# A graph product of 15 batches as seven block products, with layernorm and row sums in other bursts

## The chip, the cores and the metric

The kernel runs on one core of one Trainium2 chip. The metric is device time in microseconds (us) of one execution, lower is better. The core's engines are TensorE (PE in the profile, with its weight loads shown apart as PEld), VectorE (DVE), ScalarE (ACT), GpSimd (POOL) and SyncE (SP, which here only issues DMAs). Each engine runs its own instructions in order; they meet through semaphores. All data are float32.

## The reference

The input is x of 16 batches, each 1024 nodes (N) by 256 channels (C), and one 1024 x 1024 adjacency matrix. Layer 0 is an attention whose queries come from a graph product; layer 1 is a graph convolution with two batch norms. Cut to what matters here:

```python
fea = jnp.transpose(x, (0, 2, 1))                       # [B, C, N]
c_adj = jnp.mean(fea, axis=1)                           # mean over channels, [B, N]
diff = c_adj[:, None, :] - c_adj[:, :, None]
A = jnp.abs(jnp.abs(jax.nn.sigmoid(diff) - 0.5) - 0.5) * 2.0
Wg = adj[None] * (A + jnp.transpose(A, (0, 2, 1))) * 0.5
g = jnp.einsum('bcn,bnm->bcm', fea, Wg)                 # the graph product
q = jax.nn.relu(g * para)                               # queries
k, v = split(x @ kv_w)                                  # 4 heads of 64 channels
attn = jax.nn.softmax(q @ k.T * scale)                  # per head, 1024 x 1024
x = layernorm(x + attn @ v)
# layer 1
x = layernorm(x + batchnorm(relu(batchnorm(A_hat @ x @ W1.T)) @ W2.T))
```

The graph product of one batch is a 256 x 1024 matrix times a 1024 x 1024 matrix. It is the part that is changed.

## The kernel before

**Stages.** The attention of all 16 batches comes first, up to about 1640 us of the span. Layer 1 follows and is untouched by the change. The order of work on TensorE, ScalarE, VectorE and SP in the attention stage is written out by hand: the program's order is the order in which each of these engines (and the SP queue of DMA issues) executes. GpSimd is scheduled separately.

**Bursts.** One unit is a 128 x 1024 tile of scores (128 keys, two heads of 512 queries each). A burst is two units, and a batch has 16 bursts, numbered u = 0 to 15 (the loop at L1266). In every burst the order is: `scores` of this burst's two units (L944: matmuls into `ps`, then ScalarE's exponential into `p`), then `back`, which is `outputs` of the burst before (L960: matmuls of `p` with the values into `po`, then VectorE's running sum `acc` of `p`, L981 and L983). `ps` has two PSUM buffers of two banks each (tag "s"), `p` has four SBUF buffers. A third pair of PSUM buffers of one bank each (tag "t", `tile_t`) serves everything else. After bursts 3, 7, 11 and 15 a group of eight units is complete: in the following burst `po` is copied by ScalarE (L990), added and transposed in 32 x 32 squares by VectorE (L991, L1001), stored (L1002) and later read back as rows (L1011). `normalise` (L1013) makes the denominators with one small matmul group `den`, sends them through HBM and back to columns; `residual` (L1038) divides and adds to x, on GpSimd.

**What prepares the next batch.** While batch b's bursts run, batch b+1's (and the start of b+2's) preparation is spread over them by `prologue` (L774), which returns three lists:

- `first`: `begin` (L784) sums x over channels on VectorE (L788), stores the 1024 means to HBM in 4-byte pieces (L795) and reads them back as a row on all partitions, `crow` (L797); `transpose_squares` (L810) transposes x from a second load `xS` in 32 x 32 squares (`load_squares`, L758, four DMAs for each half of the channels, one buffer).
- `side`: for each of eight 128-row blocks, `weights_abs` (L833) and `weights_tanh` (L838) on ScalarE and `weights_adj` (L842) on VectorE, which give `wg`, the weighted adjacency. The first needs `crow`.
- `steps`: values and keys from xT (L889, L902), and the graph product (L846): for each half c of the channels, eight blocks by two halves of 512 columns, 16 matmuls into a `tile_s` pair, followed by one VectorE operation times `para` (L861) and one rectifier on ScalarE (L864).

**Where they run, for batch b:** burst 0: values and keys of b+1, side entries; bursts 1 to 3: the remaining side entries; burst 4: the layernorm of batch b-1 (`statistics_x1` and `finish_x1`), the first half of the graph product of b+1 and the last keys; burst 5: load of x and of the first squares for b+2; burst 8: `begin` and the first transpose for b+2, the second half of the graph product of b+1, `normalise`; bursts 9 to 15: side entries for b+2, one or two per burst; burst 11: `residual` and the second transpose.

Batch 0's own graph product is a separate routine (`graph_first`, L866) and stays as it is.

Of the kernel before, what the change touches and what calls it, by code (L numbers as in the profile page):

```python
# [10 lines left out]
F32 = mybir.dt.float32  # L11
I32 = mybir.dt.int32
AF = mybir.ActivationFunctionType
ALU = mybir.AluOpType
# [4 lines left out]
P = 128  # L19
# [496 lines left out]
def fast_path(  # L516
# [187 lines left out]
    H0, H1 = slice(0, HALF), slice(HALF, N)  # L704
    C0, C1 = slice(0, P), slice(P, C)
# [27 lines left out]
    with (  # L733
# [12 lines left out]
        st = {}  # L746
# [27 lines left out]
        def prologue(b):  # L774
# [6 lines left out]
            def step(f, *a):  # L781
                steps.append((f, a))
# [27 lines left out]
            def transpose_squares(c):  # L810
                if c == 0:
                    s["xT"] = xTp.tile([P, CC, N], F32, tag="xT", name=f"xT_{b}")
                nc.vector.transpose(
                    s["xT"][:, c, :], s["xS", c].rearrange("p j i -> p (j i)")
                )
                if c == 0:
                    load_squares(b, 1)

            def row_of_means():

# [22 lines left out]
                    w, w, 1.0, adj_s[:, n, :], op0=ALU.subtract, op1=ALU.mult  # L843
                )

            def graph_mm(c, n):  # L846
                if n == 0:
                    s["pg"] = tile_s(f"pg_{b}_{c}")
                    if c == 0:
                        s["qT"] = qkv.tile([P, CC, N], F32, tag="qT", name=f"qT_{b}")  # L850
                for hs in (H0, H1):
                    nc.tensor.matmul(  # L852
                        s["pg"][:, hs], xt[:, n, c * P : (c + 1) * P], s["wg", n][:, hs],
                        start=(n == 0), stop=(n == NCH - 1),
                    )
                if n == NCH - 1:
                    queries(c, slice(0, N), s["pg"])

            def queries(c, hs, ps):
                q = s["qT"][:, c, hs]  # L860
                nc.vector.scalar_tensor_tensor(  # L861
                    q, ps, -scale, para_s[:, c, hs], op0=ALU.mult, op1=ALU.mult
                )
                nc.scalar.activation(q, q, AF.Relu)  # L864
# [56 lines left out]
            for c in range(CC if b else 0):  # L921
                for n in range(NCH):
                    step(graph_mm, c, n)
            for n in range(NCH if b == 0 else 0):
                step(graph_first, n)
            for n in range(NCH):
                side.append((weights_abs, (n,)))
                side.append((weights_tanh, (n,)))
                if n:
                    side.append((weights_adj, (n - 1,)))  # L930
            side.append((weights_adj, (NCH - 1,)))
            return first, steps, side


# [136 lines left out]
        def run(fs, k):  # L1071
            for f, a in fs[:k]:
                f(*a)
            del fs[:k]
# [129 lines left out]
        with tc.manual_schedule(  # L1204
# [61 lines left out]
            for j in range(len(bursts)):  # L1266
                b, u = j // PERB, j % PERB
                for i in bursts[j]:
                    scores(i)
                if u == 0:  # L1270
                    steps, side = next_steps, next_side
                    next_first, next_steps, next_side = [], [], []
                if j:
                    back(j - 1)
                if u in (5, 9, 13):
                    run(rows_of, 1)
                if u == 5 and b + 2 < B:
                    load_x(b + 2)
                    load_squares(b + 2, 0)
                    next_first, next_steps, next_side = prologue(b + 2)  # L1280
                if b == B - 1:
                    if u == 0:
                        run(sums, 1)
                        run(rows_of, 1)
                    elif u in (2, 13):
                        run(full, 2)
                    elif u == 8:
                        run(sums, 1)
                    elif u == 3:
                        late.clear()  # L1290
                elif u == 0:
                    for i in range(7):
                        if b:
                            run(steps, 1)
                            if i < 5:
                                run(side, 2)
                        if i == 1:
                            run(sums, 1)
                            run(rows_of, 1)
                elif u < 4:  # L1300
                    if u == 1:
                        run(full, 2)
                    run(side, 2 if u < 3 else 99)
                elif u == 4:
                    run(late, 1)
                    keys_last = steps[:1] if b else []
                    del steps[: len(keys_last)]
                    for n in range(NCH):
# [610 lines left out]
```

## Time and profile before

| What | Time |
|---|---|
| median of 3 runs | 2533.0 us (2530.41 to 2534.95) |
| the profiled execution | 2533.89 us |
| its span, first to last instruction | 2532.1 us |
| its mean granted TensorE clock | 0.996 |

| Engine | busy us | share |
|---|---|---|
| VectorE | 1606.9 | 63% |
| ScalarE | 1197.5 | 47% |
| GpSimd | 415.6 | 16% |

| Line | what | count | busy us, mean ns |
|---|---|---|---|
| L973 | matmuls of p with values | 4096 | 506.6, 589 |
| L952 | matmuls of scores | 4096 | 504.9, 593 |
| L983 | VectorE, running sum of p | 384 | 505.4, 1316 |
| L842 | VectorE, weights times adjacency | 128 | 161.4, 1281 |
| L833 | ScalarE, absolute value | 128 | 146.7, 1147 |
| L838 | ScalarE, tanh | 128 | 135.8, 1061 |

A float32 matmul shows as two records, each of about half its time; four 64 x 64 matmuls share the array in L952 and L973. Matmul records overlap, so their mean durations are longer than their spacing. The second of the profile's tables splits the span in 40 slices; the DMA engines are lightly loaded in the attention stage and SP's issue order matters more than bandwidth.

### The profile page before, as it was taken

To read this page: it belongs to the slowest core of one execution; us is meant where nothing else is said; L and a number is where in the kernel's file an instruction comes from. 1 tells how busy PE (TensorE), PEld (TensorE's weight loads), DVE (VectorE), ACT (ScalarE), POOL (GpSimd) and SP (SyncE) were. 2 spreads that over 40 slices of the span, in tenths; PEclk is the share of its full clock that TensorE was granted. 3 is DMA by queue.
4 is the path that set the end of the run, shared out by engine and by line. 5 is a ranking of instruction groups with operands and counts; after the bars stand their busy time and mean duration, and the time that the engine had idled before them with its cause. 6 is when DMAs were issued, how large, how long until landed. Compare 5 with 4: busy or idle time off the path is not lost.

```text
span 2532.1 us, 32436 instructions
## 1 busy us (share of the span) xinstructions
PE 2493.3 (98%) x12646; PEld 1085.3 (43%) x12646; DVE 1606.9 (63%) x2082; ACT 1197.5 (47%) x1471; POOL 415.6 (16%) x486
## 2 busy tenths in 40 slices
PE   9999999999999999999999999999999999999997
PEld 5443443434444434434444443344444444444455
DVE  5475665765756656657657566865655566468568
ACT  6375664654755656646647555510110110144458
POOL 0011110101111111102011112431222122000026
PEclk9999999999999999999999999999999999999999
DMA  3123223132232232231322312222221222165559
GB/s 133 38 41 81 60 43 73 45 64 59 47 76 63 39 76 66 45 71 34 76 59 43 80 34 43 76 71 95 84 100 67 87 96 100 63 219 166 183 174 342
DMA packets 396978, 216.19 MB, mean 85 GB/s; under 512 B 335504, under 2 KB 368784, under 8 KB 388368
## 3 DMA queue, kind: packets, MB, share of 16 engines
q1 hardware_dynamic: 391456, 163.16, 26.0%
q0 software_dynamic: 4832, 50.34, 4.8%
q8 instruction: 101, 1.65, 0.3%
q14 instruction: 61, 0.50, 0.1%
q10 hardware_dynamic: 528, 0.52, 0.1%
HBM read 130.29 MB, written 83.69 MB: 85 GB/s over the span
## 4 chain that ended last, share of the span: by engine, by line
PE 84%; DVE 11%; DMA 2%; issue 1%; ACT 1%; SPq 1%; POOL 0%; DVEq 0%; POOLq 0%; ACTq 0%
PE ps L952 16%; PE po L973 16%; PE pg L852 15%; PE pv L902 5%; PE b_agg L1424 4%; PE pk L889 4%; PE c_agg L1424 4%; PE po L1706 3%; PE a_agg L1424 2%; PE b_h L1456 2%; PE b_o L1632 2%; PE c_h L1456 2%; PE c_o L1632 1%; PE a_h L1456 1%; PE pg L874 1%
## 5 line engine op out<-in xcount | busy, mean ns | idle before, releaser
L983 DVE TENSOR_TENSOR acc<-acc,p 128x1024 f32<-128x1024 f32 x384 | 505.4, 1316 | 146.3 <-ACT p L957 120.7
L957 ACT ACTIVATE p<-ps 128x1024 f32<-128x1024 f32 x512 | 495.9, 1021 | 155.7 <-PE ps L952 106.6
L973 PE MATMUL po<-p,v 64*64 64x512 f32 x4096 | 506.6, 589 | 1.3 <-DVE oT L991 1.3
L952 PE MATMUL ps<-qT,kT 64*64 64x512 f32 x4096 | 504.9, 593 | 2.1 <-ACT p L957 1.8
L852 PE MATMUL pg<-wg,x 128*128 128x512 f32 x960 | 420.0, 595 | 0.0
L973 PEld LDWEIGHTS po<-p,v 64*64 64x64 f32 x4096 | 172.8, 133 | 277.0 <-issue 261.5
L852 PEld LDWEIGHTS pg<-wg,x 128*128 128x128 f32 x960 | 179.9, 190 | 239.6 <-issue 215.3
L952 PEld LDWEIGHTS ps<-qT,kT 64*64 64x64 f32 x4096 | 160.2, 133 | 282.2 <-issue 217.2
L1047 POOL TENSOR_TENSOR o<-o,r_all 128x512 f32<-128x512 f32 x62 | 77.4, 1249 | 1078.5 <-DVE r_all L1041 885.3
L861 DVE SCALAR_TENSOR_TENSOR qT<-pg,para_s 128x1024 f32<-128x1024 f32 (+1 forms) x34 | 39.2, 1161 | 248.8 <-PE pg L852 246.0
L842 DVE SCALAR_TENSOR_TENSOR wg<-wg,adj_s 128x1024 f32<-128x1024 f32 x128 | 161.4, 1281 | 18.4 <-ACT wg L838 18.4
L864 ACT ACTIVATE qT<-qT 128x1024 f32<-128x1024 f32 (+1 forms) x34 | 34.2, 1009 | 264.4 <-DVE qT L861 264.4
L833 ACT ACTIVATE wg<-crow,ccol 128x1024 f32<-128x1024 f32 x128 | 146.7, 1147 | 11.4 <-DMA crow<-c 11.1
L838 ACT ACTIVATE wg<-wg 128x1024 f32<-128x1024 f32 x128 | 135.8, 1061 | 1.8
L902 PE MATMUL pv<-kvw_s,xT 128*128 128x256 f32 x512 | 123.9, 385 | 0.0
L889 PE MATMUL pk<-xT,kvw_s 128*128 128x512 f32 x256 | 121.9, 598 | 0.0
L630 ACT ACTIVATE x<-x,nm_l,rs_l 128x256 f32<-128x256 f32 x128 | 64.9, 590 | 119.9 <-POOL nm_l L626 119.9
L902 PEld LDWEIGHTS pv<-kvw_s,xT 128*128 128x128 f32 x512 | 95.0, 190 | 50.2 <-issue 28.3
L1424 PE MATMUL a_agg<-ahT,x1l 128*128 128x512 f32 x240 | 108.1, 593 | 0.7 <-ACT agg L1192 0.7
L1424 PE MATMUL b_agg<-aT,x1S 128*128 128x512 f32 x240 | 107.9, 592 | 0.0
L1048 POOL TENSOR_TENSOR x<-x,o 128x512 f32<-128x512 f32 x62 | 97.5, 1573 | 4.7
L656 ACT COPY p_agg<-a_agg 128x512 f32<-128x512 f32 x15 | 8.8, 586 | 183.3 <-PE a_agg L1424 183.3
(208 smaller groups left out, 2863.5 us busy)
## 6 DMA issues: line engine op xcount, KB each, us to landing
h<-hw POOLq DMA_DIRECT2D x16, 2048.0 KB, 6.6
hl<-h SPq DMA_DIRECT2D x32, 1024.0 KB
x<-x POOLq DMA_DIRECT2D x16, 1024.0 KB, 4.2
x1l<-x SPq DMA_DIRECT2D x16, 1024.0 KB
xf<-x SPq DMA_DIRECT2D x16, 1024.0 KB
o<-oS SPq DMA_DIRECT2D x62, 256.0 KB
o<-o SPq DMA_DIRECT2D x248, 64.0 KB
x<-in_x_dram SPq DMA_DIRECT2D x15, 1024.0 KB
```

The lines of the kernel that those rows point to most:

```text
L833: nc.scalar.activation(w, s["crow"], AF.Abs, bias=s["ccol"][:, n : n + 1])
L838: nc.scalar.activation(w, w, AF.Tanh, scale=0.5)
L842: nc.vector.scalar_tensor_tensor(w, w, 1.0, adj_s[:, n, :], op0=ALU.subtract, op1=ALU.mult)
L852: nc.tensor.matmul(s["pg"][:, hs], xt[:, n, c * P : (c + 1) * P], s["wg", n][:, hs], start=(n == 0), stop=(n == NCH - 1),)
L889: nc.tensor.matmul(ps, kvw_s[:, c, kc * P : (kc + 1) * P], s["xT"][:, c, hs], start=(c == 0), stop=(c == CC - 1),)
L902: nc.tensor.matmul(pt[:, j * C : (j + 1) * C], s["xT"][:, c, n * P : (n + 1) * P], kvw_s[:, c, C : 2 * C], start=(c == 0), stop=(c == CC - 1),
L952: nc.tensor.matmul(ps[kh * D : (kh + 1) * D, hd * HALF : (hd + 1) * HALF], kT[r, pr, ks], qT[r, pr, qh * HALF : (qh + 1) * HALF], start=Tr ...
L957: nc.scalar.activation(p, ps, AF.Exp)
L973: nc.tensor.matmul(g["po"][kh][hd * D : (hd + 1) * D, :], s["v"][r, m, h * D : (h + 1) * D], p[r, hd * HALF : (hd + 1) * HALF], start=(m = ...
L983: nc.vector.tensor_add(g["acc"], g["acc"], p)
L1424: nc.tensor.matmul(ps, left, right, start=(start and i == 0), stop=(i == NCH // 2 - 1), skip_group_check=True,)
L1456: nc.tensor.matmul(ps, left, right, start=start, stop=True, skip_group_check=True)
```

## The change

The 256 x 1024 by 1024 x 1024 product of batches 1 to 15 is written in two-by-two blocks: the left matrix in four blocks A11 to A22 (512 nodes by 128 channels), the right one in four blocks of `wg` (512 x 512: `lo` and `hi` rows, H0 and H1 columns). Seven block products replace the eight of before; each is four matmuls into one PSUM bank of tag "t". The sums that this takes are made in place by VectorE: the left ones in a buffer S that shares the one buffer of `xS`, the right ones over the blocks of `wg` themselves, in four rounds `right(1)` to `right(4)`, each as soon as the products that read the old contents are past. Products 1 and 2 add up in bank a, product 3 takes d, products 6, 7 and 4 add up in bank b, product 5 takes c. Partial results are kept in qT.

The work around it is placed anew. The load of x goes from burst 5 to 7, the first squares from 5 to 9, the second from 8 to 12; `begin` goes from 8 to 10, the two transposes from 8 and 11 to 12 and 15. The side entries of batches from 2 on go from bursts 9 to 15 and 0 to 2 to bursts 12 to 15 (three in each) and burst 0 (two with each of the first six steps), in a new order with ScalarE's entries ahead. The layernorm of the batch before is cut in four parts, in bursts 2, 3, 5 and 6.

```diff
             def transpose_squares(c):
...
-                if c == 0:
-                    load_squares(b, 1)
...
-            def graph_mm(c, n):
-                if n == 0:
-                    s["pg"] = tile_s(f"pg_{b}_{c}")
...
-                for hs in (H0, H1):
+            A11, A12 = xt[:, M0, C0], xt[:, M1, C0]
+            A21, A22 = xt[:, M0, C1], xt[:, M1, C1]
...
+            def left_first():
+                s["S"] = xsp.tile([P, 2, NCH // 2, P], F32, tag="xS", name=f"S_{b}")
+                s2, s4 = s["S"][:, 0], s["S"][:, 1]
+                nc.vector.tensor_tensor(s2, A21, A22, ALU.add)
+                nc.vector.tensor_tensor(s2, s2, A11, ALU.subtract)
+                nc.vector.tensor_tensor(s4, A12, s2, ALU.subtract)
+
+            def left_third():
+                nc.vector.tensor_tensor(s["S"][:, 1], A11, A21, ALU.subtract)
+
+            def left_last():
+                nc.vector.tensor_tensor(s["S"][:, 0], A21, A22, ALU.add)
+
+            def right(k):
+                for i in KC:
+                    dst, one, two = {
+                        1: (lo(i, H1), lo(i, H1), lo(i, H0)),
+                        2: (hi(i, H1), hi(i, H1), lo(i, H1)),
+                        3: (lo(i, H0), hi(i, H1), lo(i, H0)),
+                        4: (hi(i, H0), hi(i, H0), hi(i, H1)),
+                    }[k]
+                    nc.vector.tensor_tensor(dst, one, two, ALU.subtract)
+
+            def product(k, ps, start):
+                S = s["S"]
+                for i in KC:
+                    left, right = {
+                        1: (xt[:, i, C0], lo(i, H0)),
+                        2: (xt[:, i + NCH // 2, C0], hi(i, H0)),
+                        3: (S[:, 1, i], hi(i, H1)),
+                        4: (xt[:, i + NCH // 2, C1], hi(i, H0)),
+                        5: (S[:, 0, i], lo(i, H1)),
+                        6: (S[:, 0, i], hi(i, H1)),
+                        7: (S[:, 1, i], lo(i, H0)),
+                    }[k]
                     nc.tensor.matmul(
-                        s["pg"][:, hs], xt[:, n, c * P : (c + 1) * P], s["wg", n][:, hs],
-                        start=(n == 0), stop=(n == NCH - 1),
-                    )
-                if n == NCH - 1:
-                    queries(c, slice(0, N), s["pg"])
+                        ps, left, right, start=(start and i == 0), stop=(i == NCH // 2 - 1),
...
+            def rectify(c, hs):
+                q = q_at(c, hs)
+                nc.scalar.activation(q, q, AF.Relu, scale=-scale)
+
+            def weigh(c, hs):
+                nc.vector.tensor_mul(q_at(c, hs), q_at(c, hs), para_s[:, c, hs])
+                rectify(c, hs)
...
+            def p1():
...
+                product(1, pg["a"], True)
+                nc.scalar.copy(q_at(1, H0), pg["a"])
+                right(1)
+
+            def p3():
+                pg["d"] = tile_t(f"pgd_{b}")
+                product(3, pg["d"], True)
+                nc.scalar.copy(q_at(0, H1), pg["d"])
+                left_third()
+                right(2)
+
+            def p2():
+                product(2, pg["a"], False)
+                nc.vector.tensor_mul(q_at(0, H0), pg["a"], para_s[:, 0, H0])
+                rectify(0, H0)
+                nc.vector.tensor_add(q_at(0, H1), q_at(0, H1), q_at(1, H0))
+
+            def p6():
...
+                nc.vector.tensor_add(q_at(0, H1), pg["b"], q_at(0, H1))
+                left_last()
+
+            def p7():
+                product(7, pg["b"], False)
+                nc.vector.tensor_add(q_at(1, H1), pg["b"], q_at(1, H0))
+
+            def p5():
...
+                for c in range(CC):
+                    nc.vector.tensor_add(q_at(c, H1), pg["c"], q_at(c, H1))
+                for c in range(CC):
+                    weigh(c, H1)
+
+            def p4():
+                product(4, pg["b"], False)
+                nc.vector.tensor_add(q_at(1, H0), pg["b"], q_at(1, H0))
+                weigh(1, H0)
...
+                a, t, j = weights_abs, weights_tanh, weights_adj
+                side += [(f, (n,)) for f, n in (
+                    (a, 0), (a, 1), (t, 0), (t, 1), (a, 2), (t, 2),
+                    (a, 3), (t, 3), (a, 4), (t, 4), (a, 5), (t, 5),
+                    (a, 6), (j, 0), (t, 6), (j, 1), (a, 7), (j, 2), (t, 7), (j, 3),
+                    (j, 4), (j, 5), (j, 6), (j, 7),
+                )]
...
-                        late.append((statistics_x1, (b,)))
-                        late.append((finish_x1, (b,)))
+                        for f in (statistics_x1, finish_x1):
+                            for ns in (range(NCH // 2), range(NCH // 2, NCH)):
+                                late.append((f, (b, ns)))
...
-                if u == 5 and b + 2 < B:
+                if u == 7 and b + 2 < B:
                     load_x(b + 2)
-                    load_squares(b + 2, 0)
...
-                            if i < 5:
-                                run(side, 2)
+                            run(side, 2)
...
                     if u == 1:
                         run(full, 2)
-                    run(side, 2 if u < 3 else 99)
+                        st[b + 1]["graph"]["left"]()
+                    else:
+                        run(late, 1)
+                    run(side, 99)
                 elif u == 4:
-                    run(late, 1)
+                    p = st[b + 1]["graph"]["p"]
                     keys_last = steps[:1] if b else []
                     del steps[: len(keys_last)]
-                    for n in range(NCH):
-                        run(steps, 1)
-                        if n == 3:
-                            run(late, 1)
+                    p[1]()
+                    p[3]()
+                    p[2]()
                     run(keys_last, 1)
                 elif u == 8:
-                    run(next_first, 2)
-                    run(steps, NCH)
+                    p = st[b + 1]["graph"]["p"]
+                    p[6]()
                     run(sums, 1)
-                elif u > 8:
+                    p[7]()
+                    p[5]()
+                    p[4]()
+                elif u < 8:
+                    if u < 7:
+                        st[b + 1]["graph"]["right"](u - 2)
+                        run(late, 1)
+                else:
+                    if u == 9 and b + 2 < B:
+                        load_squares(b + 2, 0)
+                    if u == 10:
+                        run(next_first, 1)
                     if u == 11:
                         run(full, 2)
+                    if u == 12:
                         run(next_first, 1)
-                    run(next_side, 2 - u % 2)
+                        if b + 2 < B:
+                            load_squares(b + 2, 1)
+                    if u == 15:
+                        run(next_first, 1)
+                    if u > 11:
+                        run(next_side, 3)
```

More of the change, by code (lines that the diff above doesn't have):

```diff
@@ L844, in weights_adj, with lo, hi @@
                 )
-            def graph_mm(c, n):
-                if n == 0:
-                    s["pg"] = tile_s(f"pg_{b}_{c}")
-                    if c == 0:
-                        s["qT"] = qkv.tile([P, CC, N], F32, tag="qT", name=f"qT_{b}")
-                for hs in (H0, H1):
+            A11, A12 = xt[:, M0, C0], xt[:, M1, C0]
+            A21, A22 = xt[:, M0, C1], xt[:, M1, C1]
+            def lo(i, hs):
+                return s["wg", i][:, hs]
+            def hi(i, hs):
+                return s["wg", i + NCH // 2][:, hs]
@@ new lines, in prologue @@
+            KC = range(NCH // 2)
+            def left_first():
[6 more added lines that the diff above has]
+                nc.vector.tensor_tensor(s["S"][:, 1], A11, A21, ALU.subtract)
@@ L852, in graph_mm, with q_at @@
                     nc.tensor.matmul(
-                        s["pg"][:, hs], xt[:, n, c * P : (c + 1) * P], s["wg", n][:, hs],
-                        start=(n == 0), stop=(n == NCH - 1),
-                    )
-                if n == NCH - 1:
-                    queries(c, slice(0, N), s["pg"])
+                        ps, left, right, start=(start and i == 0), stop=(i == NCH // 2 - 1),
+                        skip_group_check=True,
+                    )
+            def q_at(c, hs):
+                return s["qT"][:, c, hs]
@@ new lines, in rectify @@
+            def rectify(c, hs):
[4 more added lines that the diff above has]
+                rectify(c, hs)
+            pg = {}
+            def p1():
+                s["qT"] = qkv.tile([P, CC, N], F32, tag="qT", name=f"qT_{b}")
+                pg["a"] = tile_t(f"pga_{b}")
+                product(1, pg["a"], True)
+                nc.scalar.copy(q_at(1, H0), pg["a"])
+                right(1)
@@ new lines, in p3 @@
+            def p3():
[10 more added lines that the diff above has]
+            def p6():
+                pg["b"] = tile_t(f"pgb_{b}")
+                product(6, pg["b"], True)
+                nc.vector.tensor_add(q_at(0, H1), pg["b"], q_at(0, H1))
+                left_last()
@@ new lines, in p7 @@
+            def p7():
+                product(7, pg["b"], False)
+                nc.vector.tensor_add(q_at(1, H1), pg["b"], q_at(1, H0))
+            def p5():
+                pg["c"] = tile_t(f"pgc_{b}")
+                product(5, pg["c"], True)
+                for c in range(CC):
[6 more added lines that the diff above has]
+                weigh(1, H0)
@@ L920, in prologue @@
                 step(keys, i // 2, i % 2)
-            for c in range(CC if b else 0):
-                for n in range(NCH):
-                    step(graph_mm, c, n)
             for n in range(NCH if b == 0 else 0):
                 step(graph_first, n)
[L926 to L931, printed above, removed]
+            if b < 2:
+                for n in range(NCH):
+                    side.append((weights_abs, (n,)))
+                    side.append((weights_tanh, (n,)))
+                    if n:
+                        side.append((weights_adj, (n - 1,)))
+                side.append((weights_adj, (NCH - 1,)))
+            else:
[6 more added lines that the diff above has]
+                )]
+            if b:
+                s["graph"] = dict(
+                    left=left_first, right=right,
+                    p=(None, p1, p2, p3, p4, p5, p6, p7),
+                )
             return first, steps, side
@@ L1302, in fast_path @@
                         run(full, 2)
-                    run(side, 2 if u < 3 else 99)
+                        st[b + 1]["graph"]["left"]()
+                    else:
+                        run(late, 1)
+                    run(side, 99)
                 elif u == 4:
-                    run(late, 1)
+                    p = st[b + 1]["graph"]["p"]
                     keys_last = steps[:1] if b else []
                     del steps[: len(keys_last)]
-                    for n in range(NCH):
-                        run(steps, 1)
-                        if n == 3:
-                            run(late, 1)
+                    p[1]()
+                    p[3]()
+                    p[2]()
                     run(keys_last, 1)
                 elif u == 8:
-                    run(next_first, 2)
-                    run(steps, NCH)
+                    p = st[b + 1]["graph"]["p"]
+                    p[6]()
                     run(sums, 1)
-                elif u > 8:
+                    p[7]()
[5 more added lines that the diff above has]
+                        run(late, 1)
+                else:
+                    if u == 9 and b + 2 < B:
+                        load_squares(b + 2, 0)
+                    if u == 10:
+                        run(next_first, 1)
                     if u == 11:
                         run(full, 2)
+                    if u == 12:
                         run(next_first, 1)
-                    run(next_side, 2 - u % 2)
+                        if b + 2 < B:
[4 more added lines that the diff above has]
+                        run(next_side, 3)
                 if b == B - 2:
```

## The prediction

> **What bounds the kernel now.** I read first the busy times, then the chain of waits, then the costliest groups, then one batch's timelines. The attention stage runs to about 1640 us in bursts of two score tiles, sixteen to a batch.
>
> ```profile
> PE 2493.3 (98%) x12646; PEld 1085.3 (43%) x12646; DVE 1606.9 (63%) x2082; ACT 1197.5 (47%) x1471; POOL 415.6 (16%) x486
> ...
> PE 84%; DVE 11%; DMA 2%; issue 1%; ACT 1%; SPq 1%; POOL 0%; DVEq 0%; POOLq 0%; ACTq 0%
> ...
> L957 ACT ACTIVATE p<-ps 128x1024 f32<-128x1024 f32 x512 | 495.9, 1021 | 155.7 <-PE ps L952 106.6
> ...
> L852 PE MATMUL pg<-wg,x 128*128 128x512 f32 x960 | 420.0, 595 | 0.0
> ...
> L861 DVE SCALAR_TENSOR_TENSOR qT<-pg,para_s 128x1024 f32<-128x1024 f32 (+1 forms) x34 | 39.2, 1161 | 248.8 <-PE pg L852 246.0
> ```
>
> TensorE sets the time: 98% busy, and L852 never waits. But a 47% mean for ScalarE hides how full single bursts are. Stretches of one batch and of its burst 10 (start:end, length, busy us of PE, weight loads, DVE, ACT, POOL, then granted clock, DMA share, GB/s):
>
> ```profile
> 718.10:818.40 100.30, 100.30 (x641) 42.55 (x641) 64.04 (x73) 59.46 (x70) 13.96 (x13) 1.00 0.29 59
> 739.87:743.30 3.43, 3.43 (x36) 1.22 (x32) 1.61 (x3) 3.43 (x4) 0.45 (x1) 1.00 0.36 10
> ```
>
> A batch takes 100.3 us. A plain burst takes TensorE 3.43 us, and with two exponentials (L957) and two weight activations ScalarE fills it. The SP queue and ScalarE just before:
>
> ```profile
> 722.68 0.38 SPq L795 DMA_DIRECT2D c<-ncol  x1
> 731.16 0.33 SPq L797 DMA_DIRECT2D crow<-c  x1
> 736.73 1.15 ACT L833 ACTIVATE wg<-crow,ccol 128x1024 f32<-128x1024 f32 x1
> 737.79 1.92 ACT L957 ACTIVATE p<-ps 128x1024 f32<-128x1024 f32 x2
> 739.60 1.05 ACT L838 ACTIVATE wg<-wg 128x1024 f32<-128x1024 f32 x1
> 740.54 1.14 ACT L833 ACTIVATE wg<-crow,ccol 128x1024 f32<-128x1024 f32 x1
> 741.58 1.93 ACT L957 ACTIVATE p<-ps 128x1024 f32<-128x1024 f32 x2
> ```
>
> SP's own waits over the whole span (us in total, times, longest):
>
> ```profile
> SPq L797 <- DMA c<-ncol: 136.8, 15, 10.5
> ```
>
> The row of means leaves at 722.68 and its first reader starts at 736.73: 14.05 us, of which SP waits 8 for the store (136.8/15 = 9.1 on average, 10.5 at most). Today the long burst 8 covers this.
>
> **Part 1, the products.** One half's 16 matmuls are 32 records in 13.93 us, 0.871 us a matmul. Seven products of four matmuls replace 32 by 28: 4 x 0.871 = 3.48 us a batch, all in burst 4 (12 matmuls for 16; burst 8 keeps 16). For 15 batches: -52.2 us.
>
> **Part 2, VectorE.** Added are 31 operations of 128x512: 21 sums (3 in burst 1; 4+1+4 in burst 4; 4 each in bursts 5 and 6; 1 in burst 8) and ten from PSUM or on qT. By L687's 684 ns (from PSUM) and L1609's 693 that is 21.3 us, less two L861 at 1.23: +18.9, making 83 of some 97 us. Cover: bursts 4 and 8 have over 10 us of products, and VectorE is ready long before their next reader. Bursts 5 and 6 need 2.56 (two L983) + 2.75 = 5.3 against 3.43, so VectorE falls 1.9 us behind twice; burst 7 returns 0.9 and burst 8 the rest. Four p buffers mean exp may wait for sums two bursts back: about 3.2 us of slack (sums over at 712.39, that buffer's exp at 715.59), and TensorE enters burst 8's product, which needs no p. I take 0; without cover, 2 x 1.9 = 3.8. Beside POOL the same form is slower: L702 takes 1612 ns against 683 alone. Only burst 1's three sums meet POOL's residual adds: 0 taken, up to 3 x 0.93 = 2.8. Product 7 must wait for product 6's sum out of the shared bank; the denominators' 1.00 us stands between, sum 0.69: 0, at most 0.7.
>
> **Part 3, ScalarE's copies.** Two copies (L893, 577 ns) and four 128x512 rectifies (L864's small form, 632) replace two at 1059: +1.6 us, inside bursts 4 and 8, where ScalarE has over 8 us free. Nothing.
>
> **Part 4, the row of means moves from burst 8 to burst 10.** Burst 8 keeps its length, so I use the clock above. VectorE: product 4 ends 732.0, two operations to 733.45, burst 8's first sum to 734.55, burst 9's two sums (behind their exp) to about 737.6, the reduction and two small operations 2.52 (720.13 to 722.65 now): means stored at 740.2. With 14.05 us, or 14.4 where the store is slower (1122.15 to about 1136.6): L833 can start at 754.4. It stands in burst 12, where ScalarE is free at 747.45 (scores at 743.48, exp, oT copy). ScalarE waits 7 us; behind it stand burst 13's exponentials, and TensorE waits for those, since ps has two buffers. On SP, burst 12's oS store, the second squares (four issues, 5.3 us, landing some 4 us later) and burst 13's rows (2.6) queue behind the row's wait, to about 759; their readers are burst 15's transpose, by then at 764, and burst 1's residual: nothing, though each us beyond that would be VectorE's and then the next values'.
>
> **Part 5, three weight activations a burst, 12 to 15.** Spacing by the rows: exp pair 1.81, L833 1.04 (1.18 if its reader follows), L838 0.94: a burst takes ScalarE about 4.93 us against 3.43. First activations 754.4 to 757.45; burst 13's exp, first tile out at 758.45; then 762.4 and 767.4 for bursts 14 and 15. TensorE's burst 0, due at 757.2, needs burst 15's first tile: 768.4. Stall 11.2 us. Without the late row it would be 11.2 - 6.95 = 4.25. Bounds: 4.25 (row in time) and 13.5 (store at 10.5).
>
> **Part 6, burst 0.** ScalarE arrives some 3 us late (its last three activations end at 772.3, TensorE's scores are out at 769.5): oT's copy, then VectorE's copy of the first values, hold the two PSUM banks; denominators wait some 1.3 us. I take 1.3, bounds 0 and 3 (VectorE's eight L842, 9.8 us, now all here, end 2 us behind TensorE; bursts 1 to 3 carry that and the statistics, 2.1 us each in bursts 2 and 3, on the p slack).
>
> **Part 7, the clock after the stall.** The trace has such a gap in the later stage:
>
> ```profile
> 2241.00:2244.00 3.00, 1.26 (x3) 0.20 (x2) 2.86 (x5) 0.59 (x1) 0.00 (x0) 1.00 0.81 246
> 2244.00:2247.00 3.00, 2.06 (x3) 0.80 (x4) 2.90 (x5) 0.00 (x0) 0.00 (x0) 0.79 0.25 104
> 2247.00:2250.00 3.00, 3.00 (x6) 1.39 (x5) 2.04 (x4) 0.00 (x0) 0.00 (x0) 0.64 0.00 0
> ```
>
> After some 2.4 us without matmuls the granted clock fell to 0.79 and 0.64, then returned. Missing clock there: 3 x 0.21 + 3 x 0.36 = 1.7 us. Here most of it falls where ScalarE sets the pace: I take 0.4, bounds 0 and 3.4 (twice). "TensorE: Matmul & The Clock Gate", Part 1, in the Trainium skill says an idle window of about 3.4 us halves the clock until a busy one has passed; the gap shown was shorter, the one to come, about 8 us, always qualifies. By the page, 3.4 us at half clock with no cover cost 1.7 us each time, an estimate, and the sum would be 14 x 1.3 = 18 us more.
>
> Against the store's price: "DMA: Bandwidth & Descriptors", Anatomy of one DMA, gives about 2 us of fixed cost, mostly the write receipt. The rows say 8 to 10 for this store. By the page, an estimate, the row would be 6 us sooner and the total 14 x 6 = 84 us lower. The measurement decides.
>
> **Layernorm and squares.** Statistics come after POOL's adds, whose first half is ready in 2.3 us; the applications (8 x 0.59) use the free ScalarE of bursts 5 and 6 (1.94 of 3.43 busy), so x's store on POOL's queue comes some 22 us into burst 4 and the load, now in burst 7 and behind that landing (4.2 us) on SP, still ends 10 us before burst 10 reduces x. First squares are issued behind burst 8's queue, about 731 to 736, landing before 743. Nothing; a late landing would cost what it overruns.
>
> **Sum.** Bursts 12 to 15 carry weights for batches 2 to 15, 14 times: 14 x (11.2 + 1.3 + 0.4) = 180.6; less 52.2: +128.4. The profiled execution took 2533.9 (span 2532.1 and 1.8 around it), the median is 2533.0: 2662 us. Own range 2625 to 2715.
>
> **Rivals.**
> 1. Row in time, ScalarE's surplus alone: the store lands like oS's (SP waits 3.4 us at most for that) or sooner. 14 x (4.25 + 1.3) - 52.2 = +25.5: 2559. Against it: fifteen waits averaging 9.1.
> 2. Faster: TensorE is never held in bursts 13 to 15, because ScalarE catches up within what the two ps buffers and burst 0's 13.6 us of other matmuls allow: -52, 2482. For: ScalarE is free 40 of 100 us. Against: order is fixed, and TensorE has waited for exp 136 times already. It decides below 52.2/14 = 3.7 us of stall and aftermath a batch.
> 3. VectorE becomes a second bound in bursts 0 to 8 (in-place sums slowed beside POOL, sums waiting for a product's end): 3.8 + 2.8 - 1.9 from overlaps, some 5 us a batch more: 2662 + 70 = 2732.
> 4. The product doesn't shorten, because its seven groups wait on each other in place: 3.5 us a batch back, 2714, inside my range.
>
> **How the numbers follow.** Forecast, with 4: 0.64. Rival 1 and values between it and mine: 0.15. Rival 3: 0.12. Rival 2: 0.07. Balance within 0.2%, about 5 us, what a measurement here can tell from none: 0.02. The range goes down to rival 1 and up to near rival 3: 2558 to 2725. Faster 0.07, same 0.02, slower 0.91.
>
> **What would show it.** Right: L833 in burst 12 idle some 7 us on crow, TensorE idle before L952 in bursts 13 to 15 and waiting on L957, granted clock under 1 there, a batch of about 109.7 us, L852's successor at 24.4 us a batch. Wrong: crow landing within 8 us of its means; bursts 13 to 15 at 3.4 us; or VectorE named as releaser of exp or of the products.

## The result, and the profile after

The changed kernel takes 2682.49 us (median of 4 runs, 2681.71 to 2683.23) against 2533.82: 1.0589 times as long, 95% interval 1.0571 to 1.0607. That is 148.7 us more; 128 were forecast (2662). The profiled execution has a span of 2681.3 us and a mean granted clock of 0.97. Lines below are those of the changed kernel: scores are now L1055, the exponential L1060, the absolute value L831, tanh L836, the graph product L890, the running sums L1084 and L1086.

The page of the changed kernel: busy times, the chain that ended last, and the groups that answer to those shown of before (count | busy us, mean ns | idle us just before, and what ended it):

```profile
PE 2478.7 (92%) x12526; PEld 1043.5 (39%) x12526; DVE 1867.5 (70%) x2517; ACT 1221.0 (46%) x1531; POOL 476.4 (18%) x486
...
PE 57%; DVE 20%; ACT 9%; DMA 8%; issue 4%; SPq 1%; POOL 0%; DVEq 0%; ACTq 0%; POOLq 0%
...
L1055 PE MATMUL ps<-qT,kT 64*64 64x512 f32 x4096 | 520.6, 620 | 153.3 <-ACT p L1060 153.2
...
L831 ACT ACTIVATE wg<-crow,ccol 128x1024 f32<-128x1024 f32 x128 | 144.9, 1143 | 118.4 <-DMA crow<-c 118.1
```

TensorE is busy 14.6 us less than before and idle for 8% of a longer span. The idle time stands ahead of the scores and is ended by ScalarE's exponential. Two waits of ScalarE itself have grown: for the row of means from 11 to 118 us (15 waits), and the exponential's for VectorE's running sums from 21.1 to 92.8 us (87.0 of it in 57 waits for L1086). VectorE took on 260 us. The run left_late below takes up the second wait; the first comes here. One batch in time order, SP and ScalarE:

```profile
801.39 0.38 SPq L795 DMA_DIRECT2D c<-ncol  x1
810.13 0.35 SPq L797 DMA_DIRECT2D crow<-c  x1
```

```profile
807.22 0.59 ACT L1093 COPY oT<-po 128x512 f32<-128x512 f32 x1 [0.62 <-PE po L1076]
815.22 2.19 ACT L831 ACTIVATE wg<-crow,ccol 128x1024 f32<-128x1024 f32 x2 [7.41 <-DMA crow<-c]
817.31 1.04 ACT L836 ACTIVATE wg<-wg 128x1024 f32<-128x1024 f32 x1
818.25 1.91 ACT L1060 ACTIVATE p<-ps 128x1024 f32<-128x1024 f32 x2
820.06 1.05 ACT L836 ACTIVATE wg<-wg 128x1024 f32<-128x1024 f32 x1
821.01 1.14 ACT L831 ACTIVATE wg<-crow,ccol 128x1024 f32<-128x1024 f32 x1
822.18 1.06 ACT L836 ACTIVATE wg<-wg 128x1024 f32<-128x1024 f32 x1
823.14 1.92 ACT L1060 ACTIVATE p<-ps 128x1024 f32<-128x1024 f32 x2
```

The means leave at 801.39, their first reader starts 13.8 us later. ScalarE idles 7.41 us with burst 13's exponentials queued behind that reader, then works without a gap, 4.9 us a burst (818.25 to 823.14). TensorE's timeline of the same stretch shows what that does, with the idle time in brackets:

```profile
806.99 1.90 PE L1055 MATMUL ps<-qT,kT 64*64 64x512 f32 x16
808.71 1.90 PE L1076 MATMUL po<-p,v 64*64 64x512 f32 x16
819.31 3.69 PE L1055 MATMUL ps<-qT,kT 64*64 64x512 f32 x16 [8.71 <-ACT p L1060]
...
824.67 1.89 PE L1055 MATMUL ps<-qT,kT 64*64 64x512 f32 x16
...
829.19 2.00 PE L1055 MATMUL ps<-qT,kT 64*64 64x512 f32 x16 [0.91 <-ACT p L1060]
```

Burst 13 begins at 806.99 and ends with 8.71 us of idle time; right after it burst 14's scores take 3.69 us instead of 1.90. The stretches say why (start:end, length, busy PE, weight loads, DVE, ACT, POOL, granted clock, DMA):

```profile
814.00:819.30 5.30, 0.00 (x0) 0.00 (x0) 0.01 (x1) 4.08 (x5) 0.00 (x0) 0.50 1.19 194
819.30:822.80 3.50, 3.49 (x20) 1.07 (x24) 2.44 (x2) 3.47 (x4) 0.00 (x0) 0.50 0.26 40
822.80:826.40 3.60, 3.60 (x40) 1.24 (x36) 2.12 (x2) 3.57 (x5) 0.00 (x0) 0.95 0.00 0
```

The clock fell to half in the gap and stayed there for most of the first burst after it. In the trace's clock record these spells last 10.24 us in 13 of the 14 batches, 6.83 in the other; after gaps of 8.7 to 10.1 us, 2.8 to 5.9 us of each spell fell on work.

A burst's length is the time from its first score matmul to that of the next burst. Worked out from the traces, means over batches 3 to 12, in us; bursts not listed stay at 3.43 to 3.48 in these kernels. The last five columns are experiments described below:

| Burst | before | changed | row_early | old_product_new_places | left_late | repaired | repaired_left_late |
|---|---|---|---|---|---|---|---|
| 0 | 17.46 | 18.14 | 18.14 | 18.14 | 18.14 | 17.31 | 17.22 |
| 3 | 3.43 | 3.43 | 3.43 | 3.43 | 3.43 | 3.60 | 3.43 |
| 4 | 19.19 | 16.86 | 16.86 | 19.19 | 15.76 | 17.16 | 15.76 |
| 8 | 18.47 | 18.67 | 18.67 | 18.47 | 18.67 | 18.67 | 18.72 |
| 13 | 3.55 | 13.09 | 4.81 | 13.29 | 12.98 | 3.43 | 3.43 |
| 14 | 3.44 | 5.66 | 4.89 | 5.52 | 5.40 | 3.43 | 3.43 |
| 15 | 3.46 | 4.22 | 4.99 | 4.36 | 4.48 | 3.43 | 3.43 |

Before to changed: bursts 13 to 15 +12.5, burst 0 +0.7, burst 4 -2.3, burst 8 +0.2. Fourteen times the first two and fifteen times the last two make 185 - 32 = +153 us; 149 were measured, the first and last batches being a little different.

### The profile page after: what moved, and what is told of

Read it like the earlier page. It is cut to its first block, busy times and chain, and to the rows that moved or that the text cites. A ratio compares the mean times of both kernels' runs of the same rounds, so it can differ in the third digit from the quotient of the medians.

```text
span 2681.3 us, 32690 instructions
## 1 busy us (share of the span) xinstructions
PE 2478.7 (92%) x12526; PEld 1043.5 (39%) x12526; DVE 1867.5 (70%) x2517; ACT 1221.0 (46%) x1531; POOL 476.4 (18%) x486
## 4 chain that ended last, share of the span: by engine, by line
PE 57%; DVE 20%; ACT 9%; DMA 8%; issue 4%; SPq 1%; POOL 0%; DVEq 0%; ACTq 0%; POOLq 0%
PE ps L1055 8%; PE po L1076 7%; PE pgb L890 6%; ACT p L1060 4%; DVE acc L1086 4%; PE b_agg L1545 4%; DMA c<-ncol 4%; PE pga L890 4%; PE c_agg L1545 4%; PE po L1827 3%; DVE wg L840 2%; DMA crow<-c 2%; ACT wg L831 2%; PE a_agg L1545 2%; PE b_h L1577 2%
## 5 line engine op out<-in xcount | busy, mean ns | idle before, releaser
L1055 PE MATMUL ps<-qT,kT 64*64 64x512 f32 x4096 | 520.6, 620 | 153.3 <-ACT p L1060 153.2
L1086 DVE TENSOR_TENSOR acc<-acc,p 128x1024 f32<-128x1024 f32 x384 | 507.5, 1322 | 203.0 <-ACT p L1060 179.0
L1060 ACT ACTIVATE p<-ps 128x1024 f32<-128x1024 f32 x512 | 497.7, 1018 | 205.0 <-PE ps L1055 98.2
L1055 PEld LDWEIGHTS ps<-qT,kT 64*64 64x64 f32 x4096 | 148.6, 137 | 464.6 <-ACT p L1060 260.7
L1150 POOL TENSOR_TENSOR o<-o,r_all 128x512 f32<-128x512 f32 x62 | 106.6, 1729 | 1137.9 <-DVE r_all L1144 1133.5
L1076 PEld LDWEIGHTS po<-p,v 64*64 64x64 f32 x4096 | 161.8, 136 | 296.6 <-issue 287.4
L831 ACT ACTIVATE wg<-crow,ccol 128x1024 f32<-128x1024 f32 x128 | 144.9, 1143 | 118.4 <-DMA crow<-c 118.1
L840 DVE SCALAR_TENSOR_TENSOR wg<-wg,adj_s 128x1024 f32<-128x1024 f32 x128 | 148.4, 1215 | 13.9 <-ACT wg L836 13.9
L900 ACT ACTIVATE qT<-qT 128x512 f32<-128x512 f32 x60 | 37.4, 630 | 223.9 <-DVE qT L903 151.5
L836 ACT ACTIVATE wg<-wg 128x1024 f32<-128x1024 f32 x128 | 134.9, 1054 | 1.7
L890 PE MATMUL pgb<-wg,S 128*128 128x512 f32 x240 | 111.0, 605 | 0.0
L890 PE MATMUL pga<-wg,x 128*128 128x512 f32 x240 | 109.5, 599 | 0.0
L1094 DVE TENSOR_TENSOR oT<-po,oT 128x512 f32<-128x512 f32 x64 | 44.1, 689 | 73.8 <-ACT oT L1093 72.3
L1656 ACT ACTIVATE hl<-hl,bn_sh,bn_sg 128x1024 f32<-128x1024 f32 x64 | 75.6, 1232 | 38.0 <-DMA hl<-h 35.8
```

The costliest lines, as they stand in the source:

```text
L831: nc.scalar.activation(w, s["crow"], AF.Abs, bias=s["ccol"][:, n : n + 1])
L836: nc.scalar.activation(w, w, AF.Tanh, scale=0.5)
L840: nc.vector.scalar_tensor_tensor(w, w, 1.0, adj_s[:, n, :], op0=ALU.subtract, op1=ALU.mult)
L890: nc.tensor.matmul(ps, left, right, start=(start and i == 0), stop=(i == NCH // 2 - 1), skip_group_check=True,)
L1055: nc.tensor.matmul(ps[kh * D : (kh + 1) * D, hd * HALF : (hd + 1) * HALF], kT[r, pr, ks], qT[r, pr, qh * HALF : (qh + 1) * HALF], start=Tr ...
L1060: nc.scalar.activation(p, ps, AF.Exp)
```

## The experiments

**row_early** begins the row of means in burst 8 and leaves all else as changed.

```diff
                     p[6]()
                     run(sums, 1)
+                    run(next_first, 1)
...
-                    if u == 10:
-                        run(next_first, 1)
```

> The changed kernel with one edit: the row of means is begun in burst 8, behind product 6, instead of in burst 10. My theory (the row comes late, then three weight activations a burst are too many): ScalarE no longer waits for the row in burst 12, and the stall of bursts 13 to 15 falls from 12.5 us a batch to about 4.3 to 5.5, the surplus alone; 14 batches give about 2682 - 14 x 7.5 = 2577 us (2565 to 2600). Rival, the surplus is the whole cause and the row's lateness only fills time that ScalarE would lose anyway: 2660 to 2685. Rival, VectorE's in-place sums are the bound: no change, 2670 to 2690, perhaps slower since burst 8 has more VectorE work.

Measured: 2568.18 us, 1.0139 of before (1.0122 to 1.0156). 114 us less than the changed kernel, 8.2 us a batch. ScalarE's wait for the row falls from 118.4 to 6.5 us over the span (L831's group, idle before):

```profile
L831 ACT ACTIVATE wg<-crow,ccol 128x1024 f32<-128x1024 f32 x128 | 145.1, 1145 | 6.5 <-DMA crow<-c 6.5
```

What is left in bursts 13 to 15 is 14.69 against 10.45 before: 4.24 us of surplus, which the prediction's Part 5 had at 4.25. So the late row costs two thirds of the stall and the pace one third. As the cause of this stall VectorE is out: its work is the same here, and a part of it now lies in burst 8. (The exponential's 87.0 us of waits for the running sums stand here too; left_late shows where they come from.)

**two_per_burst** leaves the row late and lowers the pace.

```diff
                     if u > 11:
-                        run(next_side, 3)
+                        run(next_side, 2)
```

> The changed kernel with one edit: two weight activations in each of bursts 12 to 15 instead of three, the rest following in bursts 0 and 1. The row stays late. My theory: the wait of 7.4 us for the row stays, each following burst costs ScalarE 1.83 + 2.1 = 3.9 us instead of 4.9, so the stall falls by about 3 us a batch; the work moved to bursts 0 and 1 costs up to 1 us there: 2682 - 14 x 2.5 = 2647 us (2635 to 2665). If the surplus were the whole cause, the stall would go almost entirely: about 2520. If VectorE's sums were the bound: 2682 or slower.

Measured: 2700.88 us, 1.0663 (1.0645 to 1.0681): slower than the changed kernel by 18 us where I had expected 35 less. Bursts 13 to 15 take 12.12, 5.47 and 3.43: 1.95 us less than in the changed kernel, not 3. And burst 3 takes 6.48 instead of 3.43, burst 4 17.54 instead of 16.86: the last two `weights_adj` (L840) came into burst 1, where VectorE's timeline shows them behind the left sums, which end at 857.3:

```profile
857.23 4.27 DVE L840 SCALAR_TENSOR_TENSOR wg<-wg,adj_s 128x1024 f32<-128x1024 f32 x2
861.43 2.54 DVE L1086 TENSOR_TENSOR acc<-acc,p 128x1024 f32<-128x1024 f32 x2
```

The running sums of burst 1 start 4.3 us later than without them, exp has no free p buffer, and TensorE stands. So my size for the work moved to bursts 0 and 1 ("up to 1 us") was wrong: it cost 3.2 us net. That raised two questions, the clock after the gap and the left sums; the next runs ask them.

**old_product_new_places** takes the kernel before, with its eight products, and moves only the row and the weights.

```diff
-                            if i < 5:
-                                run(side, 2)
+                            run(side, 2)
...
-                    run(next_first, 2)
+                    for f, a in next_first[1:2]:
+                        f(*a)
+                    del next_first[1:2]
                     run(steps, NCH)
...
-                    run(next_side, 2 - u % 2)
+                    if u == 10:
+                        run(next_first, 1)
+                    if u > 11:
+                        run(next_side, 3)
```

(with the new list of side entries for batches from 2 on)

> The kernel before (eight products, no block sums, layernorm as before) with only the row of means begun in burst 10 and the weight activations three a burst in bursts 12 to 15, the rest in burst 0. My theory: the stall comes with these two moves alone, some 12 us in bursts 13 to 15 and half a us in burst 0, 14 times: 2534 + 14 x 12.5 = 2709 us (2685 to 2725). Rival, the block product and its VectorE sums are what costs time: within 1% of 2534.

Measured: 2712.54 us, 1.0707 (1.0689 to 1.0725). Bursts 13 to 15 make 23.2 us without a single block sum; burst 0 has the same 18.14. The stall belongs to the two moves, and the product has no part in it.

**repaired** keeps the seven products and puts the row into burst 7, the weights back in their old order and pace. It also loads x in burst 5 again, and moves the layernorm's second half to burst 4 and the fourth round of right sums to burst 8; the restored list of side entries is left out below.

```diff
-                if u == 7 and b + 2 < B:
+                if u == 5 and b + 2 < B:
                     load_x(b + 2)
...
                     p[3]()
+                    run(late, 2)
                     p[2]()
...
                     p[6]()
+                    st[b + 1]["graph"]["right"](4)
...
-                    if u < 7:
-                        st[b + 1]["graph"]["right"](u - 2)
-                        run(late, 1)
+                    if u == 5:
+                        st[b + 1]["graph"]["right"](3)
+                    if u == 7:
+                        run(next_first, 1)
...
-                    if u == 10:
-                        run(next_first, 1)
                     if u == 11:
                         run(full, 2)
-                    if u == 12:
                         run(next_first, 1)
...
-                    if u > 11:
-                        run(next_side, 3)
+                    run(next_side, 2 - u % 2)
```

> The changed kernel with its seven products, but the row of means begun in burst 7, weight activations in the order and pace of the kernel before (bursts 9 to 15, one or two each), the fourth round of right sums in burst 8, the second half of the layernorm in burst 4 and x loaded in burst 5. My theory: no stall in bursts 13 to 15; the gain of 3.48 us a batch is left, less up to 1.5 for VectorE's late sums in bursts 2 to 4 and product 7's wait: 2534 - 15 x 3.48 + 15 x (0 to 1.5) = 2482 to 2505 us, faster than both kernels. Rival, VectorE is a second bound (83 of 97 us a batch) and its sums hold exp and products: 2534 or slower.

Measured: 2501.26 us, 0.9877 (0.9861 to 0.9894): faster than both kernels, 1.2% than the one before. Bursts 13 to 15 are at 3.43 each. Burst 4, at 17.16, still holds 1.4 us more than its twelve matmuls explain (19.19 - 3.48 = 15.71).

**left_late** asks where that comes from, in the changed kernel itself: the left sums go to the end of burst 3, away from GpSimd's `residual`.

```diff
                     if u == 1:
                         run(full, 2)
-                        st[b + 1]["graph"]["left"]()
                     else:
                         run(late, 1)
                     run(side, 99)
+                    if u == 3:
+                        st[b + 1]["graph"]["left"]()
```

> The changed kernel with one edit: the three left sums of a batch are made at the end of burst 3 instead of burst 1, where they run beside GpSimd's residual. My theory: burst 4 is 1.15 us longer than the twelve matmuls explain because in burst 1 these sums (0.64, 1.41, 1.65 us) and the running sums behind them (4.27 for two) are slowed by GpSimd, so VectorE lags and exp waits for a p buffer. Moved, burst 4 falls from 16.86 to about 15.7 us: 2682 - 15 x 1.15 = 2665 us (2660 to 2672). Rival, the in-place right sums or the statistics alone are too much for VectorE: 2680 or more.

Measured: 2664.51 us, 1.0524 (1.0504 to 1.0543). Burst 4 falls to 15.76. First the changed kernel: VectorE in burst 1 (L858 to L860 are the left sums; GpSimd's four operations of `residual` run from 850.60 to 857.33), and what held burst 4's second scores:

```profile
850.45 0.64 DVE L858 TENSOR_TENSOR S<-x 128x512 f32<-128x512 f32 x1
851.12 1.41 DVE L859 TENSOR_TENSOR S<-S,x 128x512 f32<-128x512 f32 x1
852.57 1.65 DVE L860 TENSOR_TENSOR S<-x,S 128x512 f32<-128x512 f32 x1
854.14 4.27 DVE L1086 TENSOR_TENSOR acc<-acc,p 128x1024 f32<-128x1024 f32 x2
```

```profile
858.50 1.02 ACT L1060 ACTIVATE p<-ps 128x1024 f32<-128x1024 f32 x1 [1.19 <-DVE acc L1086]
```

```profile
859.58 1.09 PE L1055 MATMUL ps<-qT,kT 64*64 64x512 f32 x8 [0.86 <-ACT p L1060]
```

The same three sums in left_late, away from `residual` (GpSimd has only operations of 128x8 there):

```profile
854.34 0.66 DVE L858 TENSOR_TENSOR S<-x 128x512 f32<-128x512 f32 x1
855.03 0.69 DVE L859 TENSOR_TENSOR S<-S,x 128x512 f32<-128x512 f32 x1
855.76 0.69 DVE L860 TENSOR_TENSOR S<-x,S 128x512 f32<-128x512 f32 x1
856.37 2.55 DVE L1086 TENSOR_TENSOR acc<-acc,p 128x1024 f32<-128x1024 f32 x2
```

Now only the two running sums of burst 1 stand beside `residual`, and take 3.21 us instead of 4.27. The exponential's waits for L1086 fall from 87.0 us to 0.6. The edit changes two things at once, though: the sums leave GpSimd's neighbourhood, and their own 2.0 us leave burst 1. How much the place alone was worth, no run shows. An estimate from the rows: at 2.04 us for the sums and 2.56 for two running sums, burst 1's work would have ended 7.7 us after that burst's scores began (847.33), even in the old place. In left_late the statistics behind it start 7.5 us after those scores (840.05 to 847.55), held by GpSimd's operations. So nearly all of the gain would be the slowing.

**repaired_left_late** makes the same edit in the repaired kernel.

> The repaired kernel with the same one edit, left sums at the end of burst 3. My theory: bursts 3 and 4 lose their 0.17 and 1.45 us of waiting, 15 times: 2501 - 24 = 2477 us (2473 to 2487), close to the whole gain of 52 us less 0.2 us a batch for product 7's wait. Rival, VectorE's total of work in bursts 1 to 4 is the limit wherever it stands: 2495 to 2503.

Measured: 2479.08 us, 0.979 (0.9775 to 0.9805): 2.1% less. That is 54 us faster than before, where the matmuls saved account for 52. TensorE is 98% busy again, and the idle time ahead of the scores is gone (the repaired kernel's lines; L1046 are the scores):

```profile
PE 2439.7 (98%) x12526; PEld 1049.2 (42%) x12526; DVE 1845.8 (74%) x2517; ACT 1218.5 (49%) x1531; POOL 467.2 (19%) x486
...
L1046 PE MATMUL ps<-qT,kT 64*64 64x512 f32 x4096 | 494.8, 592 | 2.4 <-ACT p L1051 2.4
```

**kept_warm** puts eight matmuls that nobody reads into the gap of two_per_burst.

```diff
                         run(next_side, 2)
+                    if u == 13 and b + 2 < B:
+                        keep = tile_t(f"keep_{b}")
+                        for i in range(8):
+                            nc.tensor.matmul(
+                                keep, kvw_s[:, 0, :P], kvw_s[:, 0, :HALF], start=True, stop=True,
+                            )
```

> The kernel with two activations a burst, with eight matmuls added in burst 13 whose product nobody reads, so that TensorE is busy while ScalarE waits for the row. If half the granted clock after the gap is what kept that kernel's stall above its ScalarE pace: bursts 14 and 15 lose some 1.2 us a batch and the time falls by about 17 us, 2701 to 2684 us, granted clock 0.99 instead of 0.968. If the clock is hidden there: 2701, whatever the clock shows. If the added matmuls hold TensorE themselves: more than 2701.

Measured: 2680.52 us, 1.0585 (1.0562 to 1.0607): 20.4 us less with 7 us more of matmuls in each of 14 batches. First a stretch of two_per_burst, in burst 14 of a batch, then two of this kernel, from bursts 13 and 14 of the same batch:

```profile
824.00:828.00 4.00, 4.00 (x20) 1.03 (x20) 2.73 (x3) 3.90 (x5) 0.00 (x0) 0.50 0.44 54
```

```profile
814.00:818.00 4.00, 2.84 (x21) 0.75 (x23) 1.75 (x2) 4.00 (x6) 0.00 (x0) 1.00 1.07 125
818.00:822.00 4.00, 4.00 (x40) 1.17 (x36) 2.73 (x3) 3.97 (x5) 0.00 (x0) 1.00 0.09 14
```

The clock stays at 1.00 here, as in these bursts of 13 of the 14 batches (the mean over the span is 0.989, since the stall in burst 3 still brings it down). Burst 14 falls from 5.47 to 3.86 us, ScalarE's pace, and burst 15 rises from 3.43 to 3.90. So the fallen clock was what the pace of two a burst ran into: 20.4 / 14 = 1.5 us a batch by the times, 1.2 by bursts 13 to 15 of the two traces.

**changed_kept_warm** does the same in the changed kernel.

> The changed kernel with the eight matmuls in burst 13 whose product nobody reads. Here three activations a burst follow the late row, and ScalarE is busy without a gap from the row's landing to burst 0, so half the clock should be hidden: 2682 us, within 6 (0 to 0.4 us a batch), though the granted clock rises from 0.97 to 0.99. If the clock's fall costs this kernel what it cost the one with two a burst: some 17 to 20 us faster, 2663.

Measured: 2681.85 us, 1.0588 (1.057 to 1.0606): no difference, with the mean granted clock at 0.995 instead of 0.97 (5 of the 14 batches still have a short spell at half). Bursts 14 and 15 only trade (5.01 and 4.87 for 5.66 and 4.22). With three activations a burst ScalarE is later than a TensorE at half clock, so the clock is hidden.

**no_block_sums** and **no_block_sums_small** leave out 18 of the 21 block sums.

```diff
             def left_third():
-                nc.vector.tensor_tensor(s["S"][:, 1], A11, A21, ALU.subtract)
+                pass
...
             def left_last():
-                nc.vector.tensor_tensor(s["S"][:, 0], A21, A22, ALU.add)
+                pass
...
-                    nc.vector.tensor_tensor(dst, one, two, ALU.subtract)
+                    pass
```

> The changed kernel without the 18 block sums of bursts 4 to 8 (the four rounds of right sums, the third and the last left sum); it leaves them out, so its products are not the graph product. My theory: those sums are covered, product groups wait on them by 0.2 us at most, and the stall of bursts 13 to 15 is untouched: 2672 to 2684 us. Rival, VectorE's in-place sums bound the changed kernel: 50 us or more faster, under 2635.

Measured: 7207.35 us, a miss of another kind. Without its sums the product gives scores so large that the kernel's limit on the softmax denominators is passed, and it computes everything a second time by its general path; the total says nothing about the sums. In the attention stage of its trace the bursts are those of the changed kernel (burst 4 16.86, 13 to 15 13.13, 5.61, 4.27). The second of the two adds one edit, which makes the queries a thousand times smaller:

```diff
-                nc.scalar.activation(q, q, AF.Relu, scale=-scale)
+                nc.scalar.activation(q, q, AF.Relu, scale=-scale * 1e-3)
```

> As the kernel without the 18 block sums, which leaves them out, but with the queries scaled down a thousand times in the rectifier, so that the softmax stays within the limit below which the kernel doesn't compute everything a second time. My theory: 2675 to 2684 us, the sums of bursts 4 to 8 are covered. Rival, VectorE's in-place sums bound the changed kernel: under 2635.

Measured: 2681.94 us, 1.059 (1.0572 to 1.0608). Taking 18 sums a batch away, some 12 us of VectorE's time, changes nothing: they are covered.

## Why the prediction was right

The sign, the mechanism of bursts 13 to 15 and most sizes held. Per batch, in us:

| Part | forecast | measured | shown by |
|---|---|---|---|
| 1 products | -3.48 | -3.43 | left_late, burst 4: 19.19 to 15.76 |
| 2 VectorE's sums beside GpSimd | 0 (up to 2.8) | +1.10 | left_late, burst 4: 16.86 to 15.76 |
| 2 right sums and the rest | 0 (up to 3.8) | 0 | no_block_sums_small |
| 2 wait of product 7 | 0 (up to 0.7) | +0.2 | burst 8 |
| 4 row too late | 6.95 | 8.3 | row_early |
| 5 three a burst | 4.25 | 4.24 | row_early |
| 6 burst 0 | 1.3 | 0.7 | burst 0 |
| 7 clock | 0.4 | 0 | changed_kept_warm |

Two terms were mis-sized, the rest were within 0.6. Over all batches of the traces the left sums cost 15 us that the sum didn't have, the row 16 more than its term and product 7 another 3, while burst 0 cost 8 less and the clock 6 less. That the total came within 20 us is in part luck, since misses cancel.

**The left sums beside GpSimd** were the term I took at 0 with 2.8 as its bound. I counted the sums' own excess and found the p buffers' slack enough. What I left out is that the running sums behind them fall into the same stretch and are slowed as well, 4.27 us for two instead of 2.56; both together used up the slack and held burst 4's scores by 1.1 us, 14 times (batch 0's burst 4 shows no such wait). The Trainium skill has the rule, which I didn't weigh: "SBUF — State Buffer", Who interferes with whom, says that a VectorE instruction with two SBUF inputs contends with a GpSimd instruction that reads SBUF, because both need the same read interface. The rows agree: 0.66 to 0.69 us away from `residual`, 1.41 and 1.65 beside it, and 0.64 for the first one, which began 0.15 us before GpSimd's operation.

**The row** came later than computed by 1.3 us a batch. In the batch shown the means left 8.2 us after burst 9's scores began (793.21 to 801.39), not 7.2. The working took the end of product 4 from the clock of before, where the denominators' matmuls (`den`) stand between the product and burst 9's scores at 732.95. In the changed kernel they stand behind product 6, and product 4 (L890) runs right up to burst 9's scores at 793.21. First a line of before, then one of the changed kernel:

```profile
731.96 1.06 PE L1020 MATMUL den<-acc,ones 128*32 128x512 f32 x8
```

```profile
789.68 3.60 PE L890 MATMUL pgb<-wg,x 128*128 128x512 f32 x8
```

So all that VectorE does between product 4 and the means came 1.0 us later. The rest is the store and the load behind it: from the means to their first reader 14.45 us on average over batches 2 to 13, where the working had 14.2 (740.2 to 754.4). SP's wait for the store was 9.3 us on average (111.7 us in 12 waits in the queue's own list), not the 2 us that the prediction set beside its rows. Nor did its other estimate of that kind come, 18 us more for a clock without cover: changed_kept_warm shows no difference.

Of the rivals, the first (row in time, surplus alone, 2559) is what row_early turned out to be, at 2568, the 9 us between them being about burst 4's 1.1 fourteen times and burst 8's 0.2 fifteen times, less burst 0's 0.6 fourteen times. The second, ScalarE catching up so that TensorE is never held, is refuted by the burst lengths of 4.8 to 5.0 us in row_early. The third, VectorE as a second bound at 2732, was there, but only with 1.1 us a batch. The fourth, products that wait on each other, is 0.2 us a batch. What was named as evidence came out: L831 idle 7.4 us on the row, scores held by the exponential in bursts 13 to 15, a granted clock of half there, a batch of 111.1 us on average (110.3 in the one shown) against 109.7. One of the signs of being wrong came as well: VectorE is named as releaser of the exponential, for 92.8 us where it was 21.1 before. TensorE lost the 1.1 us a batch by it. Only the clock was wrongly feared in this kernel, and rightly in two_per_burst, where Part 7's price of up to 1.7 us uncovered was 1.2 to 1.5.

## What to carry to other kernels

A mean share of busy time doesn't show whether a step can move: set the work of the engine against the length of the very burst that receives it, and where two engines hand a buffer pair back and forth, a burst that is over by 1.5 us is paid nearly in full (4.24 us for three such bursts). Before a load is moved towards its reader, count the whole way from the first instruction that feeds it, with the wait for a small store in it; the seven products were worth their 52 us only when the row was begun three bursts sooner, the weight activations had their old pace and the left sums had moved. Keep two-input VectorE work out of the stretch in which GpSimd reads the same memory, and count what queues behind it too.

## What the runs showed of the hardware

- A store of 1024 four-byte pieces to HBM held SP for up to 10.5 us before its reader could be issued: 9.1 on average in the kernel before (136.8 us in 15 waits), 9.3 in the changed one (111.7 in 12).
- After 8.7 to 10.1 us without matmuls (the changed kernel) the granted clock was 0.50, and it stayed there for 2.8 to 5.9 us of work. Gaps of 2.9 us, in burst 3 of two_per_burst, were enough for a spell at 0.50 in 11 of 14 batches.
- Eight matmuls that nobody reads, put into the gap, kept the clock at 1.00 in 13 of 14 batches of one kernel and made it 20 us faster. In another they did so in 9 of 14, and its time didn't change.
- Two-input sums of 128x512 on VectorE, 0.66 to 0.69 us away from GpSimd's `residual`, took up to 1.65 us beside it.
